# Seven block products in a gated cell: a first sum held in three PSUM tiles, the fifth product's bank reused, the second sum moved behind the sixth

## Chip, core and metric

One core of a Trainium2 chip runs the whole problem. The metric is the device time in microseconds, the median of three runs: 1669.55 us (1669.16 to 1672.69). The names of engines are those of the profile: PE is TensorE's matmul, PEld its weight load, DVE is VectorE, ACT is ScalarE, POOL is GpSimd, SP the queue that issues most DMAs.

## What is computed

The input is `x`, 64 graphs of 256 nodes with 256 features, and `adj`, 64 matrices of 256 x 256. After a layer norm and a ReLU, each graph goes through two convolutions along the nodes, through a message product with an affinity matrix, and then through a gated cell, which is where the change lies. All is in float32.

```
h = max(layernorm(x), 0)
x_conv = relu(bn(conv17(relu(bn(conv1(h))))) + h)
A = exp(-dist(h @ w_se)) * adj
x_nmp = A @ relu(h @ w_msg + b_msg)
gi = concat(x_conv, x_nmp) @ w_ih.T + b_ih        # 768 columns: r, z, n
gh = h @ w_hh.T + b_hh
r = sigmoid(gi_r + gh_r);  z = sigmoid(gi_z + gh_z)
n = tanh(gi_n + r * gh_n)
out = x + (1 - z) * n + z * h
```

## The kernel before

**Work and stages.** Two graphs (G = 2, 512 columns side by side) are a pair; 32 pairs are taken in 8 blocks of four. Features lie on the partitions, in two halves of 128. The wide convolution is done with a hand-written transform, whose additions run on DVE; its products stream filter weights from DRAM into the slots `wb`. A block's loop body (lines 1331 to 1495) lists, pair by pair, embedding, affinity, aggregation, convolution, `sums` and `gates`.

**The seven products.** A gate's pre-activation for a pair is a 2 x 2 block product: two feature halves in, two out (dc 0 and dc 1), with the two graphs as the other block index. It is done with seven block products in place of eight (`seven`, line 1162). `sums` (line 1104) forms the block sums of the inputs on DVE in slots of `wb`; `weight_sums` forms those of the weights once, in `w_x`. One call of `part(p, k, ...)` (line 1140) is product k, added up over the inputs h, xn and xc into 512 columns of PSUM: the 256 columns of one gate and the 256 of the other. `seven` is called for the gates r and z (unit RZ, three inputs for each of two gates, six matmuls a part) in all 32 pairs, and for n (unit NH, three matmuls a part) in the first 31; the last pair has an order of its own (lines 1237 to 1253), which the change leaves alone.

**Where the sums lie.** PSUM is cut into four tiles of one bank, `aux`, and two tiles of two banks, `acc`; both are rings that hand out tiles in the order of the program text (lines 580 and 581). In `seven`, `A` and `E` are `acc` tiles and the fifth product `p5` an `aux` tile. The steps are: product 1 into `A[:, 0]`; ACT writes its negative into `E[:, 0]`; product 5 into `p5`, which ACT copies to the slot `e`; product 2 onto `A[:, 0]`; product 6 onto `E[:, 0]`; DVE adds `E[:, 0]` and `e` into `A[:, 1]` (line 1174, below "the add"); product 7 onto `E[:, 0]`, which the add has just read; DVE writes `E[:, 1]` (line 1176); product 3 onto `A[:, 1]`; product 4 onto `E[:, 0]`. `opened(0, A)` and `opened(1, E)` then read both graphs of one half at a time: for RZ two ACT tanh of 128x512 each (`rz`, line 1192), for NH an ACT affine and an ACT copy of 128x512 each (`n`, line 1197).

**What sets the order.** All operations go through a recorder (line 250). Before they are emitted, a planner (line 395) orders each engine's instructions by simulated time from a table of costs: at each moment an engine takes what is ready, by due time (`late`), so a matmul of another stage can be put where the next one would wait. Due times on PE follow the text. For PSUM the planner knows only whole tiles (lines 279 and 280), so the two banks of an `acc` tile are one thing to it. On the chip each engine then runs its own list in order. `between` (line 1424 and the like) is work listed between RZ and NH of a pair: in the first and third pair of a block it holds `affinity` (line 1027), which takes four `aux` tiles at once for four small matmuls (`zT`), recorded as one task; ACT then takes four exponentials from them and DVE four products with `adj`.

All recorded operations are shown at line 378 (those small matmuls at 374), so groups are told apart by the tiles they write and read: `acc<-wb,w_x` is product 7, `aux<-wb,w_x` product 5, `acc<-hT,w_x`, `acc<-xnm,w_x` and `acc<-Yv,w_x` product 3, `acc<-wb,w_hh` and `acc<-wb,w_ih` products 6 and 4, `acc<-hT,w_hh` and its like products 1 and 2. The profile counts each float32 matmul as two records.

## Time and profile before

| | |
|---|---|
| median of three runs | 1669.55 us |
| profiled execution, its own time | 1671.88 us |
| span of the profiled execution | 1670.1 us |
| PE busy | 1645.7 us, 99% of the span |
| DVE busy | 1456.8 us, 87% |
| ACT busy | 1127.2 us, 67% |
| POOL busy | 236.0 us, 14% |
| mean granted TensorE clock | 0.997 |
| product 7, PE idle before its matmuls | 7.8 us |

The span runs from the first to the last instruction; 1.8 us of the profiled execution's time lie around it. "Busy" is the sum of the times in which an engine has at least one instruction running; for PE the ends are modelled, so a start that comes late can show partly as busy time of the matmul before it. "Idle before" is the time in which the engine had nothing running just ahead of an instruction, with the instruction whose signal ended it.

### The profile page before, as it was taken

What the parts mean: (1) busy time and instruction counts of PE and PEld (TensorE: products, weight loads), DVE (VectorE), ACT (ScalarE), POOL (GpSimd) and SP (SyncE); (2) the same over time, 40 slices, a digit from 0 to 9 for tenths busy, and PEclk for the clock granted to TensorE, in tenths of its full rate; (3) what the DMA queues carried; (4) which work ended last, traced back from release to release, by engine and by line L of the source; (5) the groups of instructions that cost most, each with busy time, mean ns of one, the idle gap of its engine ahead of it and who ended that gap; (6) DMA issues with size and microseconds to landing.
All of it is one profiled execution on the core that took longest, in us unless ns stands there. A gap on an engine that the chain in (4) does not pass through costs nothing.

```text
span 1670.1 us, 26281 instructions
## 1 busy us (share of the span) xinstructions
PE 1645.7 (99%) x8984; PEld 1413.3 (85%) x8984; DVE 1456.8 (87%) x3401; ACT 1127.2 (67%) x2029; POOL 236.0 (14%) x245
## 2 busy tenths in 40 slices
PE   9999999999999999999999999999999999999997
PEld 6888878978899788988889887897889978898886
DVE  7979989889889898898998988988988989789544
ACT  5546766776767767686756776677676776657554
POOL 4210210022110221103110131002211022000000
PEclk9999999999999999999999999999999999999999
DMA  9882557856468455783478654684647845375022
GB/s 250 301 291 75 135 109 203 264 110 147 108 202 227 105 123 126 237 205 95 114 139 265 151 122 103 176 259 110 146 108 207 222 108 133 83 231 142 16 61 51
DMA packets 314936, 261.37 MB, mean 156 GB/s; under 512 B 192875, under 2 KB 240263, under 8 KB 314802
## 3 DMA queue, kind: packets, MB, share of 16 engines
q1 hardware_dynamic: 297010, 216.71, 48.9%
q0 software_dynamic: 17376, 42.66, 11.3%
q8 instruction: 71, 1.16, 0.3%
q14 instruction: 63, 0.52, 0.1%
q10 hardware_dynamic: 416, 0.32, 0.1%
HBM read 156.60 MB, written 43.78 MB: 120 GB/s over the span
## 4 chain that ended last, share of the span: by engine, by line
PE 70%; DVE 24%; DMA 3%; issue 2%; ACT 1%; SPq 0%; DVEq 0%; ACTq 0%
PE acc L378 49%; PE aux L378 21%; DVE V L378 5%; DVE tr L378 3%; DVE U L378 3%; DVE T L378 3%; DVE wb L378 3%; DVE acc L378 2%; DVE gn L378 2%; DMA wb<-filt 2%; DVE st L378 1%; DVE PT L378 1%; DVE msg L378 1%; PE aux L374 1%; DVE Sv L378 0%
## 5 line engine op out<-in xcount | busy, mean ns | idle before, releaser
L378 PE MATMUL acc<-wb,w_ih 128*128 128x256 f32 x768 | 191.9, 379 | 0.0
L378 PEld LDWEIGHTS acc<-wb,w_ih 128*128 128x128 f32 x768 | 145.9, 190 | 19.8
L378 POOL DMA_DIRECT2D back<-in_x_dram x62 | 56.5, 1051 | 727.7 <-ACT back L378 379.5
L378 POOL TENSOR_TENSOR rstd<-rstd,neg_half 128x4 f32<-128x4 f32 x32 | 85.8, 2682 | 458.5 <-DVE shift L378 272.5
L378 PE MATMUL acc<-wb,w_x 128*128 128x256 f32 x576 | 136.9, 383 | 7.8 <-DVE acc L378 7.8
L378 ACT COPY back<-tr 128x512 uint16<-128x512 uint16 x124 | 128.3, 1078 | 22.5 <-DVE tr L378 22.2
L378 DVE SCALAR_TENSOR_TENSOR V<-T,V 128x128 f32<-128x128 f32 (+2 forms) x448 | 141.1, 379 | 0.0
L378 PE MATMUL aux<-wb,w_x 128*128 128x256 f32 x576 | 138.1, 382 | 0.0
L378 PEld LDWEIGHTS acc<-wb,w_x 128*128 128x128 f32 x576 | 106.9, 190 | 36.3 <-DVE acc L378 17.7
L378 PEld LDWEIGHTS aux<-wb,w_x 128*128 128x128 f32 x576 | 108.7, 191 | 17.3 <-DVE wb L378 2.6
L378 PE MATMUL aux<-w_msg,hT 128*128 128x259 f32 x512 | 121.7, 381 | 0.0
L378 PE MATMUL acc<-V,wb 128*128 128x128 f32 x1024 | 118.5, 275 | 0.8 <-DMA wb<-filt 0.8
L378 PEld LDWEIGHTS acc<-U,wb 128*128 128x128 f32 x1024 | 116.9, 192 | 2.6 <-ACT acc L378 1.7
L378 PE MATMUL acc<-U,wb 128*128 128x128 f32 x1024 | 117.2, 275 | 1.6 <-DMA wb<-filt 1.6
L378 PEld LDWEIGHTS acc<-V,wb 128*128 128x128 f32 x1024 | 116.4, 192 | 1.3 <-DMA wb<-filt 1.2
L378 ACT ACTIVATE gn<-acc,bn_columns 128x512 f32<-128x512 f32 (+1 forms) x64 | 43.5, 680 | 106.6 <-PE acc L378 101.5
L378 PE MATMUL acc<-Yv,w_ih 128*128 128x256 f32 x380 | 108.4, 381 | 2.1 <-ACT Yv L378 2.1
L378 PE MATMUL acc<-wb,w_hh 128*128 128x256 f32 x384 | 109.4, 380 | 0.7 <-ACT acc L378 0.7
L378 PEld LDWEIGHTS aux<-w_msg,hT 128*128 128x128 f32 x512 | 96.5, 190 | 14.3
L378 ACT COPY back<-gn 128x1024 uint16<-128x1024 uint16 x62 | 82.8, 1342 | 36.3 <-DMA gn<-back 36.3
L378 PE MATMUL aux<-hT,w_c 128*128 128x512 f32 x224 | 106.1, 592 | 0.0
L378 PE MATMUL acc<-hT,w_hh 128*128 128x256 f32 x380 | 104.0, 380 | 0.0
(200 smaller groups left out, 3898.3 us busy)
## 6 DMA issues: line engine op xcount, KB each, us to landing
wb<-filt SPq DMA_DIRECT2D x348, 256.0 KB
back<-in_x_dram POOLq DMA_DIRECT2D x62, 256.0 KB, 5.0
out_dram<-back POOLq DMA_DIRECT2D x62, 256.0 KB, 2.9
x<-in_x_dram SPq DMA_DIRECT2D x58, 256.0 KB
halves_d<-halves SPq DMA_DIRECT2D x28, 512.0 KB
adjh<-halves_d SPq DMA_DIRECT2D x112, 128.0 KB
hh<-halves SPq DMA_DIRECT2D x108, 128.0 KB
filt<-Yv POOLq DMA_DIRECT2D x18, 224.0 KB, 4.4
```

The lines of the kernel that those rows point to most:

```text
L374: self.tasks[k].call.append(lambda: method(*args, **kw))
L378: self.tasks.append(Task(engine, [lambda: method(*args, **kw)], cost, size, self.first))
```

## The change

The first sum's two graphs no longer share an `acc` tile. `a0` is the first bank of an `acc` tile (its second bank stays unused), and `a1` is the `aux` tile that held the fifth product: once ACT has copied it to `e`, the add writes its sum over it. Product 2 moves behind product 6 and the add in the text. The readers of the first half then have two separate tiles to read, so each of their ACT instructions of 128x512 becomes two of 128x256. `E` stays as it was.

```diff
     def seven(i, unit, opened):
 
-        A = acc()
-        part(A[:, 0], 1, i, unit, True)
+        a0 = acc()[:, 0]
+        part(a0, 1, i, unit, True)
         E = acc()
-        nc.scalar.mul(E[:, 0], A[:, 0], -1.0)
-        p5 = aux()
-        part(p5, 5, i, unit, True)
+        nc.scalar.mul(E[:, 0], a0, -1.0)
+        a1 = aux()
+        part(a1, 5, i, unit, True)
         e = slots[ROLE["e"]].rearrange("p c d -> p (c d)")
-        nc.scalar.copy(e, p5)
-        part(A[:, 0], 2, i, unit)
+        nc.scalar.copy(e, a1)
         part(E[:, 0], 6, i, unit)
-        nc.vector.tensor_add(A[:, 1], E[:, 0], e)
+        nc.vector.tensor_add(a1, E[:, 0], e)
+        part(a0, 2, i, unit)
         part(E[:, 0], 7, i, unit)
         nc.vector.scalar_tensor_tensor(E[:, 1], E[:, 0], -1.0, e, op0=ALU.mult, op1=ALU.subtract)
-        part(A[:, 1], 3, i, unit)
-        opened(0, A)
+        part(a1, 3, i, unit)
+        opened(0, (a0, a1))
         part(E[:, 0], 4, i, unit)
         opened(1, E)
 
-    def halfs(p, k):
-        return p[:, :, k * N:(k + 1) * N]
-
-    def pieces(t):
-        return t.rearrange("p (g n) -> p g n", n=N)
+    def halfs(t, p, k):
+        if isinstance(p, tuple):
+            return [(t[:, g * N:(g + 1) * N], p[g][:, k * N:(k + 1) * N]) for g in range(G)]
+        return [(t.rearrange("p (g n) -> p g n", n=N), p[:, :, k * N:(k + 1) * N])]
...
         def rz(dc, p):
             for gate, t in ((0, tr[:, dc]), (1, tz[dc])):
-                nc.scalar.activation(pieces(t), halfs(p, gate), AF.Tanh,
-                                     bias=b_rz[:, gate * DC + dc:gate * DC + dc + 1], scale=0.5 - dc)
+                for o, v in halfs(t, p, gate):
+                    nc.scalar.activation(o, v, AF.Tanh, bias=b_rz[:, gate * DC + dc:gate * DC + dc + 1],
+                                         scale=0.5 - dc)
 
         def n(dc, p):
             g = gn[:, dc]
-            nc.scalar.activation(pieces(g), halfs(p, 1), AF.Identity,
-                                 bias=b_hh[:, 2 * DC + dc:2 * DC + dc + 1], scale=1.0 - 2 * dc)
+            for o, v in halfs(g, p, 1):
+                nc.scalar.activation(o, v, AF.Identity, bias=b_hh[:, 2 * DC + dc:2 * DC + dc + 1],
+                                     scale=1.0 - 2 * dc)
             x = XNM[i][:, dc]
-            nc.scalar.copy(pieces(x), halfs(p, 0))
+            for o, v in halfs(x, p, 0):
+                nc.scalar.copy(o, v)
```

## The prediction, as made before the result was known

> **What bounds the kernel now.** I read the shares of busy time first, then the waits of PE, then the row of product 7, and last the timeline around one of its waits. The first three lines are from the page: busy time, and the chain of work that ended last.

> ```profile
> PE 1645.7 (99%) x8984; PEld 1413.3 (85%) x8984; DVE 1456.8 (87%) x3401; ACT 1127.2 (67%) x2029; POOL 236.0 (14%) x245
> ...
> PE 70%; DVE 24%; DMA 3%; issue 2%; ACT 1%; SPq 0%; DVEq 0%; ACTq 0%
> ...
> L378 PE MATMUL acc<-wb,w_x 128*128 128x256 f32 x576 | 136.9, 383 | 7.8 <-DVE acc L378 7.8
> ```

> PE has 24.4 us without work in 1670.1, so it is the bound nearly throughout, and no edit that leaves its matmuls alone can win more than that. The chain's 24% for DVE doesn't contradict it: DVE is nearly as full, and the chain runs through it where PE starts late by tenths of a microsecond. The waits of PE itself (waiter, what ended the wait, total us, times, longest) say what the 24.4 us hold:

> ```profile
> PE acc L378 <- DVE acc L378: 7.8, 18, 0.7
> PE aux L378 <- DVE U L378: 3.6, 2, 3.4
> PE acc L378 <- DMA wb<-filt: 2.4, 2, 1.6
> PE acc L378 <- ACT Yv L378: 2.1, 1, 2.1
> ```

> The largest, 7.8 us in 18 waits, is the idle time of product 7's row: it overwrites `E[:, 0]` and must wait until the add has read it. One such place, PE and DVE in the timeline (start, duration, then the group):

> ```profile
> 950.46 1.89 PE L378 MATMUL acc<-wb,w_ih 128*128 128x256 f32 x8
> ...
> 952.11 0.75 DVE L378 BATCH_NORM_STATS2 st<-x 128x6 f32<-128x256 f32 x2
> ...
> 952.28 0.71 PE L374 MATMUL aux<-zT 9*128 9x256 f32 x8
> 952.77 0.69 DVE L378 TENSOR_TENSOR acc<-acc,wb 128x512 f32<-128x512 f32 x1
> ...
> 953.51 0.70 PE L378 MATMUL acc<-wb,w_x 128*128 128x256 f32 x2 [0.52 <-DVE acc L378]
> ```

> Product 6 ends at about 952.2; DVE, busy with statistics, starts the add at 952.77 and ends it at 953.46, and product 7 starts at 953.51. Between lie only the four small `zT` matmuls. At another place the planner found a wider filler:

> ```profile
> 966.99 0.59 PE L378 MATMUL acc<-wb,w_ih 128*128 128x256 f32 x2
> ...
> 967.42 1.88 PE L378 MATMUL aux<-hT,w_c 128*128 128x512 f32 x4
> 967.70 0.70 DVE L378 TENSOR_TENSOR acc<-acc,wb 128x512 f32<-128x512 f32 x1 [2.98 <-PE acc L378]
> ...
> 969.14 1.46 PE L378 MATMUL acc<-wb,w_x 128*128 128x256 f32 x6
> ```

> Here the add starts 0.28 us after the sixth product, is over at 968.40, and PE doesn't stop.

> [...]

> **The move of product 2.** It is 12 records in RZ and 6 in NH, PE only, without a DMA or another queue. The matmul starts of product 4 give the price of one product:

> ```profile
> 958.80 1.03 PE L378 MATMUL acc<-wb,w_hh 128*128 128x256 f32 x4
> 959.66 1.89 PE L378 MATMUL acc<-wb,w_ih 128*128 128x256 f32 x8
> 961.39 0.59 PE L378 MATMUL acc<-hT,w_hh 128*128 128x256 f32 x2
> ```

> 961.39 - 958.80 = 2.59 us for RZ, so half, 1.30 us, for NH. Moved between 6 and 7 it covers the add. The two kernels' instruction lists as built let me count what stands there. Before, of the 64 sets of seven (the last pair's included), 47 have 1.30 us or more of other matmuls, 16 have only the `zT` group and one a single transpose. That is 17 short covers for 18 waits, so of 47 covers of 1.30 us or more just one was too short. After, all 64 have at least 1.30 us: 32 exactly 2.59 (RZ), 18 exactly 1.30, 14 more than 1.30 by a filler besides. The need is about 1.1 us where DVE is free (0.28 to the start, 0.70, some 0.1 back) and 1.3 at the place above. So I take the 7.8 us down to about 0.6: 18 covers at the bare 1.30, some 3 of them short by 0.2. Gain 7.2 us. The fillers that stood there aren't lost, they only run elsewhere on a full PE.

> **Products 1, 5 and 6.** Product 6 now follows 5 with nothing between. It needs ACT's negation of the first sum; so did product 2 before, at the same place, so the wait isn't new. In NH the cover is product 5, 1.30 us, against 0.2 + 0.59 + 0.1 = 0.9 us for the negation (586 ns in its row); 20 sets of NH stand so bare in the new list. It also needs the block sums of the inputs from DVE 1.30 to 2.59 us sooner after product 5 than before; these follow the previous pair's product 4, with 5.2 us of products 1 and 5 between, for 3.5 us of DVE work (six sums, 3 x 0.68 + 3 x 0.42). Bounds: 0 and 20 x 0.3 = 6 us; I take 0.5, since the planner puts in fillers where it sees a wait, and its 47 covers were nearly all enough.

> **The bank of product 5.** Before, `p5` was free once ACT had copied it; now it is held through 6, 2, 7 and 3 and their readers, some 11.5 us in RZ (4 x 2.59 + 1.1). The ring's fourth next user is the last tile of the affinity group, so `zT` waits for the readers of `a1`: the list shows it moved from between 6 and 7 to the middle or the end of product 4. Those readers take 0.2 + 2 x 0.47 = 1.1 us after product 3, and product 4 offers 1.3 to 2.6 us. I price it at 0, cover named; without it 16 waits of up to 1.1 us. In return `a0`'s `acc` tile frees after product 2's readers instead of product 3's; I count nothing for that, as no wait on `acc` tiles of any size is in the list of waits.

> **ACT.** 64 tanh more (32 RZ) and 62 affines and copies (31 NH). Busy time: 64 x (2 x 0.474 - 0.685) + 31 x (0.948 - 0.687) + 31 x (2 x 0.405 - 0.578), with 405 ns from the 256-column copy `V<-acc`, = 16.8 + 8.1 + 7.2 = 32 us. ACT goes from 67% to 69%. None of it is on PE's path while its results come before PE needs the tile; the readers of `a0` can even start two products earlier. DVE: the same number of adds at the same price, 0.

> **The sum.** 1671.88 - 7.2 + 0.5 = 1665.2 us for an execution like the profiled one. That is 6.7 us, or 0.4%; from the median of the runs, 2.3 us lower than the profiled one, 1669.55 - 6.7 = 1662.8 us. A change under 0.2% (3.3 us) a measurement of this kernel can't tell from none.

> **Rivals.** *The add is late anyway* (same): at the 18 bare covers DVE's list decides. If it is behind by 0.3 us in each, 5 us come back, and 1667.8 us is left. For it: DVE is 87% busy, and the add above started 0.5 us late. Against: 25 covers of 1.30 us before made hardly a wait. *ACT at the seam of RZ and NH* (slower): in two pairs of four `zT` now ends beside product 4, so behind it ACT holds two tanh of 512 for dc 1 (0.575 us apart), four exponentials (1.21 us together) and then NH's negation; before, the exponentials were over two products earlier. By rows the negation ends 3.0 us after product 4, PE needs it at 3.3 to 3.5. If one copy of `adj` (1.35 us) or of the affine results gets ahead of it, PE waits 0.9 us; in 16 seams 14.4 us, and the end is 1662.8 + 14.4 = 1677.2 us. It decides from 16 waits of 0.42 us on, that is from ACT 0.8 us late at each. Against: the new list puts negation ahead of the fourth exponential and of those copies. *More gain* (faster still): in the last block PE waits 2.1 us for `Yv` and then runs 3.4 us at half clock; a shifted order could spare that, 1662.8 - 4 = 1658.8 us. The list still has that wait, so little for it. That the change doesn't do what it says is excluded by the list.

> **Chances.** Forecast 0.63, late add 0.18, seam 0.14, more gain 0.05. Faster by over 0.2%: 0.68; within: 0.18; slower: 0.14. The range leaves out the seam and the far end of more gain: 1658.5 to 1669.5; the forecast's own is 1660 to 1666.

> **What would show it.** Product 7's row with under 1.5 us of idle time and the first line of PE's waits gone; `tr<-acc` and `tr<-aux` of 256 at about 474 ns; ACT near 69%; PE's busy time unchanged within 3 us. Wrong it would be if PE shows a new wait on ACT (`acc<-acc` ahead of product 6, or the readers of `a1` ahead of `zT`) of 3 us or more in total, or if product 7 still waits for the add.

## The result, and the profile after

The changed kernel takes 1672.78 us (median of 20 runs, 1667.02 to 1677.49), the kernel before 1670.06 us on the same chip (20 runs, 1668.98 to 1672.69). The ratio is 1.0016, with a 95% interval of 1.0009 to 1.0022: 2.7 us slower, where 6.7 us faster had been forecast. The profiled execution of the changed kernel happens to be the shortest of its 20: 1667.02 us, near the 1665.2 us that the prediction's sum gave for an execution. The loss lies in the others, so I profiled the same kernel three times more (1672.17, 1670.68 and 1674.83 us) and read all four.

The page of the changed kernel, first profile, with the lines that answer those of before, and the rows of products 5 and 6:

```profile
PE 1644.6 (99%) x8984; PEld 1411.5 (85%) x8984; DVE 1459.5 (88%) x3401; ACT 1146.3 (69%) x2155; POOL 242.6 (15%) x245
...
PE 75%; DVE 16%; DMA 4%; issue 2%; ACT 2%; SPq 1%; POOL 1%; ACTq 0%; DVEq 0%
...
L378 PE MATMUL aux<-wb,w_x 128*128 128x256 f32 x576 | 137.1, 380 | 2.2 <-DVE wb L378 2.2
L378 PE MATMUL acc<-wb,w_x 128*128 128x256 f32 x576 | 135.1, 380 | 0.0
...
L378 PE MATMUL acc<-wb,w_hh 128*128 128x256 f32 x384 | 105.0, 382 | 5.1 <-ACT acc L378 3.1
```

Product 7's row has no idle time left (7.8 us before). The time before products 5 (2.2 us) and 6 and 4 (5.1 us, which were 0.7 before) is new. The waits of PE in the same profile (waiter, what ended the wait, total us, times, longest):

```profile
PE acc L378 <- ACT acc L378: 3.1, 1, 3.1
PE aux L378 <- DVE wb L378: 2.2, 6, 0.5
...
PE acc L378 <- DVE acc L378: 1.9, 4, 0.9
```

The third line was the 7.8 us of the add. It now holds other waits: product 4 behind the write of `E[:, 1]`. The place that the change was meant for looks as the prediction drew it (PE and DVE in the timeline):

```profile
945.22 1.13 PE L378 MATMUL aux<-wb,w_x 128*128 128x256 f32 x4 [0.28 <-DVE wb L378]
...
948.78 1.03 PE L378 MATMUL acc<-hT,w_hh 128*128 128x256 f32 x4
...
949.42 0.70 DVE L378 TENSOR_TENSOR aux<-acc,wb 128x512 f32<-128x512 f32 x1
...
951.37 0.81 PE L378 MATMUL acc<-wb,w_x 128*128 128x256 f32 x3
```

The add runs from 949.42 to 950.12 while product 2 runs (948.78 to 951.37), and product 7 follows it without a stop. But product 5 has just waited 0.28 us for an input sum.

**Where the time went.** Since the ends of matmuls are modelled, I took all starts on PE, subtracted from each distance the usual one (0.216 us a record of 256 columns, 0.429 of 512, 0.112 of 128), and put every excess of more than 0.1 us down to the product that came late. A wait counts here with some 0.1 us more than its idle time: the add's 18 waits, 7.8 us by idle time, are 9.6. Means in us:

| excess ahead of | before, 2 profiles | after, first profile | after, 3 further | `after_late` (below) |
|---|---|---|---|---|
| product 7 (the add) | 9.6 | 0.0 | 0.4 | 0.0 |
| product 5 (input sums) | 0.9 | 3.3 | 3.9 | 1.0 |
| products 6 and 4 | 1.0 | 6.0 | 6.8 | 0.6 |
| TensorE at half clock | 1.2 | 0.0 | 2.3 | 1.3 |
| `zT` and fixed places | 15.8 | 15.9 | 16.5 | 15.3 |
| all the rest | 14.2 | 13.3 | 14.1 | 13.7 |
| sum | 42.7 | 38.5 | 44.0 | 31.9 |
| own time of these executions | 1671.2 | 1667.0 | 1672.6 | 1661.0 |

The sums move as the times do (+1.3 against +1.4 from before to the three further profiles). So the 9.2 us that were to be won were won, and 3.0 + 5.8 + 1.1 us came in at products 5, 6 and 4 and by the clock.

**Product 6 in the first block.** ACT and PE in the second pair, first profile after:

```profile
201.89 1.35 ACT L378 COPY back<-gn 128x1024 uint16<-128x1024 uint16 x1 [3.83 <-DMA gn<-back]
...
203.54 1.36 ACT L378 COPY hT<-hh 128x1024 uint16<-128x1024 uint16 x1 [0.30 <-DMA hh<-halves]
...
204.44 1.46 PE L378 MATMUL aux<-wb,w_x 128*128 128x256 f32 x6
...
204.76 0.68 ACT L378 ACTIVATE tr<-acc,b_rz 128x512 f32<-128x512 f32 x1
...
207.09 1.34 ACT L378 COPY back<-gn 128x1024 uint16<-128x1024 uint16 x1
...
208.39 0.60 ACT L378 ACTIVATE acc<-acc 128x512 f32<-128x512 f32 x1
...
209.04 0.70 PE L378 MATMUL acc<-wb,w_hh 128*128 128x256 f32 x2 [3.15 <-ACT acc L378]
```

ACT stands idle 3.83 us for a transfer (`gn<-back`), with the tanh of RZ's second half and the negation listed behind. RZ's second half was complete on PE at 199.6, and its tanh starts at 204.76. Four wide copies of about 1.3 us are then ahead of the negation, which starts at 208.39; product 5 has ended at about 205.7, and PE stands still for 3.15 us. The same two ACT instructions in the kernel before:

```profile
198.44 1.33 ACT L378 COPY back<-gn 128x1024 uint16<-128x1024 uint16 x1
...
207.98 0.58 ACT L378 ACTIVATE acc<-acc 128x512 f32<-128x512 f32 x1
```

There the copy ran 9.5 us ahead of the negation. SP had issued that transfer at 192.80; after the change it issues it at 194.22, behind a transpose of `hh` at 190.29 in place of 186.21, because ACT gives the normalised `hh` at 187.7 to 190.3 in place of 184.1 to 186.2. ACT itself waits there 1.86 us for `shift` from POOL, whose instruction ends at 187.67 (177.97 before; times on POOL are rough). The transfer took 7.7 us from issue to the copy, against at most 5.6.

**Product 4 in the later blocks.** SP, DVE and PE, second profile of the same changed kernel (`again`):

```profile
606.56 0.63 SPq L378 DMA_DIRECT2D x<-in_x_dram  x1
...
612.08 0.43 DVE L378 BATCH_NORM_STATS2 st<-x 128x6 f32<-128x256 f32 x1 [1.90 <-DMA x<-in_x_dram]
...
612.44 1.02 PE L378 MATMUL aux<-hT,w_c 128*128 128x512 f32 x2
...
613.82 0.69 DVE L378 SCALAR_TENSOR_TENSOR acc<-acc,wb 128x512 f32<-128x512 f32 x1
...
614.57 0.70 PE L378 MATMUL acc<-wb,w_hh 128*128 128x256 f32 x2 [1.11 <-DVE acc L378]
```

DVE is held 1.90 us by the statistics, whose `x` has not landed. Behind them in its list stand a short step of the transform, two input sums and then the write of `E[:, 1]`, which frees `E[:, 0]` for product 4. PE's fillers are over before that, and it waits 1.11 us. The place comes back in five later blocks (near 414, 612, 810, 1008 and 1206 us). In all four profiles of the change PE's wait there is DVE's wait for `x` less about 0.8 us (1.99 gives 1.20, 1.02 gives 0.23), and none where `x` was late by less than that.

The kernel before has the same statistics at the same place of DVE's list, four instructions ahead of the write, and DVE doesn't wait there (SP and DVE):

```profile
603.45 0.70 SPq L378 DMA_DIRECT2D x<-in_x_dram  x1
...
611.17 0.42 DVE L378 BATCH_NORM_STATS2 st<-x 128x6 f32<-128x256 f32 x1
```

So DVE's order is not what is new. The load takes about as long as before: by its semaphore it has landed 5.2 us after its issue there (608.62) and 5.5 us after it in `again`. But SP issues it at 606.56 in place of 603.45, behind a transpose of `hh` that holds SP for 5.68 us (4.90 before), while DVE comes to the statistics at 610.18 in place of 611.17. A margin of 2.5 us (611.17 - 608.62) has become a wait of 1.90.

### The profile page after: what moved, and what is told of

It reads as the page before. It is cut to its first block, busy times and chain, and to the rows that moved or that the text cites. A ratio compares the mean times of both kernels' runs of the same rounds, so it can differ in the third digit from the quotient of the medians.

```text
span 1665.2 us, 26516 instructions
## 1 busy us (share of the span) xinstructions
PE 1644.6 (99%) x8984; PEld 1411.5 (85%) x8984; DVE 1459.5 (88%) x3401; ACT 1146.3 (69%) x2155; POOL 242.6 (15%) x245
## 4 chain that ended last, share of the span: by engine, by line
PE 75%; DVE 16%; DMA 4%; issue 2%; ACT 2%; SPq 1%; POOL 1%; ACTq 0%; DVEq 0%
PE acc L378 48%; PE aux L378 26%; DVE V L378 4%; DVE T L378 3%; DMA x<-in_x_dram 2%; DVE wb L378 2%; DMA hh<-halves 1%; SPq L378 1%; PE aux L374 1%; DVE tr L378 1%; DVE Yv L378 1%; DVE e L378 1%; DMA wb<-filt 1%; DVE U L378 1%; DVE st L378 1%
## 5 line engine op out<-in xcount | busy, mean ns | idle before, releaser
L378 PE MATMUL acc<-wb,w_ih 128*128 128x256 f32 x768 | 188.9, 380 | 0.0
L378 PEld LDWEIGHTS acc<-wb,w_ih 128*128 128x128 f32 x768 | 145.3, 190 | 21.8 <-issue 2.3
L378 POOL DMA_DIRECT2D back<-in_x_dram x62 | 56.7, 1059 | 732.6 <-ACT back L378 592.7
L378 POOL TENSOR_TENSOR rstd<-rstd,neg_half 128x4 f32<-128x4 f32 x32 | 79.2, 2474 | 431.8 <-DVE shift L378 273.7
L378 DVE SCALAR_TENSOR_TENSOR V<-T,V 128x128 f32<-128x128 f32 (+2 forms) x448 | 141.4, 383 | 0.0
L378 ACT COPY back<-tr 128x512 uint16<-128x512 uint16 x124 | 130.2, 1076 | 15.7 <-DVE tr L378 15.3
L378 PE MATMUL aux<-wb,w_x 128*128 128x256 f32 x576 | 137.1, 380 | 2.2 <-DVE wb L378 2.2
L378 PE MATMUL acc<-wb,w_x 128*128 128x256 f32 x576 | 135.1, 380 | 0.0
L378 PEld LDWEIGHTS aux<-wb,w_x 128*128 128x128 f32 x576 | 108.6, 190 | 22.1 <-DVE wb L378 5.0
L378 PEld LDWEIGHTS acc<-wb,w_x 128*128 128x128 f32 x576 | 109.0, 190 | 18.6 <-issue 1.7
L378 PEld LDWEIGHTS acc<-U,wb 128*128 128x128 f32 x1024 | 118.2, 192 | 2.3 <-DMA wb<-filt 1.1
L378 PE MATMUL acc<-U,wb 128*128 128x128 f32 x1024 | 119.0, 275 | 0.9 <-DMA wb<-filt 0.9
L378 PE MATMUL aux<-w_msg,hT 128*128 128x259 f32 x512 | 118.6, 381 | 0.0
L378 PE MATMUL acc<-V,wb 128*128 128x128 f32 x1024 | 118.5, 275 | 0.0
L378 PEld LDWEIGHTS acc<-V,wb 128*128 128x128 f32 x1024 | 116.4, 192 | 0.5 <-DMA wb<-filt 0.4
L378 PE MATMUL acc<-wb,w_hh 128*128 128x256 f32 x384 | 105.0, 382 | 5.1 <-ACT acc L378 3.1
L378 PEld LDWEIGHTS aux<-w_msg,hT 128*128 128x128 f32 x512 | 95.9, 190 | 14.1
L378 DVE TENSOR_TENSOR e<-e,adj 128x256 f32<-128x256 f32 x128 | 68.8, 595 | 44.2 <-ACT e L378 43.9
L378 PE MATMUL aux<-hT,w_c 128*128 128x512 f32 x224 | 105.0, 593 | 0.1
L378 PE MATMUL acc<-Yv,w_ih 128*128 128x256 f32 x380 | 102.7, 379 | 2.1 <-ACT Yv L378 2.1
L378 PE MATMUL acc<-hT,w_hh 128*128 128x256 f32 x380 | 104.6, 381 | 0.0
L378 PE MATMUL acc<-xnm,w_ih 128*128 128x256 f32 x380 | 103.5, 379 | 0.0
```

What stands on the lines that cost most here:

```text
L378: self.tasks.append(Task(engine, [lambda: method(*args, **kw)], cost, size, self.first))
```

## The experiments

My theory was that the planner's lists are at fault: it takes a transfer as landed 1.1 us after its data have passed (`plan`, line 445), puts instructions that wait for transfers ahead of others on ACT and DVE in that trust, and the shifted lists of the change have less slack where the trust is wrong. The rivals: the split readers on ACT cost the time; the ring of tiles does (`a1` held for longer); or the half-clock stretches do, with waits as before. Where an expectation uses letters, P stands for the planner's figure being too early for any kernel, D for the waits in the lists, S for the split readers, C for the clock.

**`again`**: the changed kernel, unaltered.

> The changed kernel, unaltered, to see an execution nearer its median than the one profiled first (span 1665.2 us, the fastest of 20; the 20 ran from 1667.0 to 1677.5, those of before from 1669.0 to 1672.7). Theory D (late transfers): in the new order ACT copies and DVE statistics that wait for transfers stand ahead of the negation, of the input sums or of the write of E[:, 1], so a transfer that lands 1 to 3 us later than the planner thought reaches PE. It expects a span of 1669 to 1675 us, with product 7 still nearly free of waits (under 1.5 us), and 4 to 8 us more PE waits on ACT and DVE ahead of products 5, 6 and 4 than in the fast execution. Theory C (clock): the same waits as in the fast execution, and one to four more stretches at half clock[...]. Theory S (split readers): every execution pays, no difference between a fast and a slow one is explained.

Measured: 1672.17 us (21 runs, 1669.01 to 1677.53), ratio 1.0012 (1.0005 to 1.0019). The small loss is real, and so is the spread: 8.5 us here and 10.5 in the first series, against 3.7 to 6.7 for the kernel before.

**`tiles_only`**: the three tiles, with product 2 ahead of 6 as it was.

```diff
+        part(a0, 2, i, unit)
         part(E[:, 0], 6, i, unit)
         nc.vector.tensor_add(a1, E[:, 0], e)
-        part(a0, 2, i, unit)
```

> Three tiles as in the change, but product 2 ahead of product 6 in the text, as before. As built, 60 of 64 adds have 1.3 us or more of other matmuls behind them, 4 have less, none of the zT sort; product 6 again has product 2 between it and product 5 wherever the planner likes. If it is the move of product 2 that takes the slack from what product 6 waits for (D in its narrow form), this gives 1662 to 1665 us with a scatter of under 4 us. If the lost time comes from what the tiles do to the order of ACT and SP (D in its wide form), or from the split readers (S), it stays at 1670 to 1675 us with the scatter of the change.

Measured: 1680.1 us (1679.74 to 1681.04), ratio 1.0058 (1.0044 to 1.0071). PE's waits:

```profile
PE aux L378 <- ACT e L378: 8.0, 12, 1.0
```

Without the move, product 5 of NH gets the tile of a `zT` that has just been made, and waits until ACT has taken the exponential from it: eight of the twelve waits and 7.3 of the 8.0 us are of this kind. Product 7's wait for the add is nearly gone here too (2.6 us by starts), so what the tiles cost in this order is more than the 10 us of loss: by starts product 5 has 9.0 us of excess and product 1 and its like 7.1, where the kernel before has 0.9 and 2.3. In the change itself none of this is seen.

**`split_only`**: the kernel before, with the readers of the first half split.

```diff
-        opened(0, A)
+        opened(0, (A[:, 0], A[:, 1]))
```

(with the new `halfs`, `rz` and `n` of the change)

> The kernel before with its first half's readers split into two graphs each, nothing else: 126 more ACT instructions, tiles and text order as before. Theory S: 3 us or more slower than before, 1673 us or over. Theory D: within 2 us of before either way, ACT about 19 us busier, product 7 waiting for the add as before (about 8 us).

Measured: 1671.79 us (13 runs, 1670.44 to 1674.5), ratio 1.0012 (1.0003 to 1.002). ACT has 1141.0 us busy, the add's waits are the 7.8 us in 18 of the kernel before, and there is no new wait at product 6 above 1.2 us. The split costs about 1.7 us by the medians, too little for the 9 us that came in.

**`after_late`**: the change, with the planner taking each transfer as landed 1.5 us later.

```diff
-                t.done = self.dma + 1.1
+                t.done = self.dma + 2.6
```

> The change, with a planner that believes every transfer lands 1.5 us later than it did, so that it puts what waits for transfers later in the lists of ACT and DVE. Theory D: the waits of ACT, DVE and PE that go back to transfers shrink, the scatter falls to that of before (4 us over all runs), and the median comes to 1662 to 1667 us. Theories S and C: 1671 to 1675 us, as the change.

Measured: 1659.72 us (1658.73 to 1661.02), ratio 0.9937 (0.9924 to 0.9949), the fastest version of all. The same place in the first block:

```profile
201.25 0.68 ACT L378 ACTIVATE wb<-acc,b_rz 128x512 f32<-128x512 f32 x1
202.12 1.35 ACT L378 COPY back<-gn 128x1024 uint16<-128x1024 uint16 x1 [0.19 <-DMA gn<-back]
...
206.32 0.62 ACT L378 ACTIVATE acc<-acc 128x512 f32<-128x512 f32 x1
...
207.00 0.70 PE L378 MATMUL acc<-wb,w_hh 128*128 128x256 f32 x2 [0.33 <-ACT acc L378]
```

The transfer is no earlier (202.1 against 201.9): SP issues it at 194.45. But RZ's tanh now stand ahead of the copy that waits for it, and the negation ends 2.05 us sooner (206.94 against 208.99), though product 5 starts 0.77 us later; 0.33 us of wait are left of 3.15. The waits for transfers, first of `after_late`, then of the change:

```profile
ACT back L378 <- DMA gn<-back: 9.5, 11, 3.7
DVE st L378 <- DMA x<-in_x_dram: 4.3, 2, 3.6
```

```profile
ACT back L378 <- DMA gn<-back: 18.4, 10, 3.8
DVE st L378 <- DMA x<-in_x_dram: 12.0, 9, 3.7
```

The kernel before has 36.3 us (15) and 4.6 us (3) in these lines: more waiting for `gn<-back` than either, at no loss. So not their sum counts, but what is listed behind them.

In the later blocks it is SP's list that differs: here SP issues `x` at 596.86, ahead of the transpose of `hh` at 598.27, and the statistics at 606.25 find it landed. It is so in all five blocks. Of the 12.1 us between the last two columns of the table above, 9.1 are at products 5, 6 and 4.

**`before_late`**: the same edit of the planner in the kernel before.

> The kernel before with the planner that lands every transfer 1.5 us later: the control to the change with that planner, which took 1659.7 us. The change's own worth, once transfers are no matter, is the difference of the two. Theory D with the prediction's step for the add right: before has little to gain from this planner, since its waits on PE are the 7.8 us for the add, so it stays at 1666 to 1671 us and keeps these waits; the change's worth is then 7 to 10 us. If the late planner alone is what gained (theory P), this gives 1660 to 1663 us and the change is worth nothing.

Measured: 1677.13 us (1674.2 to 1678.14), ratio 1.0037 (1.0025 to 1.005), slower where I had expected faster or no change. Its waits:

```profile
PE acc L378 <- DVE acc L378: 5.7, 17, 0.7
...
PE aux L378 <- DVE wb L378: 3.9, 7, 0.9
```

The add's waits are still there, product 5's are new, and by starts it has 4.8 us at half clock. So the later figure isn't better as such (P falls): it is worth 12.5 us to the changed kernel (1672.17 to 1659.72) and costs the one before 7. The pair of lists and change is what counts.

**`after_late_x` and `after_late_rest`**: the later landing for the loads of `x` alone, and for all other transfers alone.

```diff
-                t.done = self.dma + 1.1
+                t.done = self.dma + 1.1 + (1.5 if k in self.slow else 0.0)
```

(`self.slow` holds the transfers into `x`, or all others)

> The change, with only the loads of x believed 1.5 us later (they are waited for by the statistics on DVE, ahead of the input sums and of the write of E[:, 1]). Theory D says that two kinds of lateness reach PE: statistics behind x on DVE (some 6 us of PE waits in the steady blocks) and copies behind hh and gn on ACT (3 us in the first block). If x is the main one: median 1663 to 1667 us, the repeating waits before products 4 and 5 gone, the 3 us wait of product 6 in the first block still there. If not: 1669 us or over.

> The complement: all transfers but the loads of x believed 1.5 us later. If x is the main cause: 1667 to 1671 us, with statistics still waiting 10 us or more for x on DVE. If the copies on ACT are: 1662 to 1665 us.

Measured: 1667.32 us (14 runs, 1663.75 to 1671.68), ratio 0.9989 (0.9981 to 0.9997), and 1662.64 us (1659.66 to 1664.61), ratio 0.9953 (0.9941 to 0.9964). With `x` alone the waits that come back in each block are gone, and product 6's wait in the first block stays (3.5 us). The rest alone gives most of the gain. But the pair doesn't part the kinds of transfer cleanly. With the rest alone SP too issues `x` ahead of the transpose of `hh` (599.88 and 601.27), so DVE's waits for `x` fall to 5.5 us in 4, though the figure for `x` is that of the change; with `x` alone the statistics stand behind the write of `E[:, 1]` instead (631.50 and 617.46).

**`after_later`**: all transfers 3.0 us later.

```diff
-                t.done = self.dma + 1.1
+                t.done = self.dma + 4.1
```

> The change, with every transfer believed 3 us later. Theory D: waits on transfers are gone already with 1.5 us, so no more is won, 1658 to 1664 us, by what the planner loses in other places for having to put copies later. A median under 1657 us would say that 1.5 us was not enough of a margin.

Measured: 1672.32 us (19 runs, 1669.8 to 1674.14), ratio 1.0013 (1.0006 to 1.0019). A miss. The waits of DVE for `x` are as few as in `after_late` (4.1 us in 2), but the starts hold 11.6 us more than there, for 12.0 us more in the profiled executions. Of these 3.7 us are in the groups of `zT`: in eight of them (one in `after_late`) PE stops between the four small matmuls, six times for ACT's copies of their input, and the group at 493.73 takes 1.29 us in place of 0.71. Products 5, 6 and 4 have 1.6 us more, the half clock 1.5, product 1 and its like 1.2, and the rest is in small pieces. More margin is not better; the lists differ everywhere.

**`after_late_b0` and `after_late_b1`**: the 1.5 us for the transfers issued up to the end of the first block, and for those of the later blocks.

> The change, with the transfers of the prologue and the first block alone believed 1.5 us later; from the second block on the lists are almost those of the change. Theory D: the 3 us wait of product 6 in pair 1 (ACT's negation behind copies whose transfers landed late) shrinks to 1.5 us or less and with it goes the half-clock stretch that it can bring, so the median falls by 3 to 5 us to 1667 to 1669 us, and the scatter (8 to 10 us in the change) to 5 us or less; the repeating waits before products 4 and 5 stay. Against D: no difference, 1671 us or over.

> The complement: the first block planned as in the change, later blocks with transfers believed 1.5 us later. Theory D: the 3 us wait of pair 1 stays, with its half-clock stretch in a part of the executions, so the scatter stays at 7 us or more; the waits repeated in each block (about 1 us a block, six blocks) go, and the median is 1663 to 1667 us. The two parts' gains should come to about the 12.5 us of the whole.

Measured: 1668.18 us (19 runs, 1664.15 to 1673.85), ratio 0.9984 (0.9975 to 0.9993), and 1664.92 us (1664.24 to 1668.3), ratio 0.9973 (0.9961 to 0.9984). The first loses the 3 us wait of product 6, and keeps product 5's 4.2 us and the waits for `x`; the second the other way round (product 6's is 2.8 us, product 5 has 0.8). From `again`, 4.0 and 7.3 us, of 12.5 for both: the two parts nearly add up (11.3). I had the spread wrong: it stays at 9.7 us in the first, and is 4.1 in the second (7 runs only). It seems to go with the later blocks.

**`tiles_only_late`**: `tiles_only` with the 2.6 us of `after_late`.

> Three tiles, product 2 ahead of product 6, and the planner that lands every transfer 1.5 us later. With the planner as it was, this kernel took 1680.1 us, and its waits were not on transfers but on the exponentials of the affinity group, whose tile product 5 of NH takes next (8.0 us in 12 waits). If moving product 2 behind the add is what spares that, this stays at 1670 us or over with these waits, against 1659.7 us for the change with this planner; if the tiles alone are what counts and the 1680 us were late transfers, it comes to 1660 to 1665 us.

Measured: 1690.0 us (1688.13 to 1690.89), ratio 1.0116 (1.0102 to 1.013), and the exponential's waits are still there (7.3 us in 8). Beside `after_late` only the place of product 2 in the text differs, with the lists that the planner makes from it, and that is 30 us; the exponential's waits are a part of it, and the rest isn't traced here.

**`look2`, `look3`, `b0_look2`, `before_look2`**: one further profile each of the change (twice), of `after_late_b0` and of the kernel before, to tell waits from clock.

> A third look at the change, unaltered, for what an execution above the fastest holds. Theory C (clock carries most of the loss): two or three stretches at half clock before the tail, and waits of PE like those of the fastest execution. Theory D (late transfers carry it): one stretch or none more, and 4 us or more of added PE waits on ACT and DVE before products 4, 5 and 6. [...]

> A fourth look at the change, unaltered, with the same expectations as the third: C wants half-clock stretches and unchanged waits, D wants 4 us or more of added waits before products 4, 5 and 6.

> A second look at the change with the first block's transfers alone believed later, whose executions still scattered over 9.7 us, to see what varies. D: the waits in the repeating blocks (before products 4 and 5) differ from look to look by 1 us or more each; C: half-clock stretches differ, the waits don't.

> A second look at the kernel before. D and C both expect its waits to be those of the first look within 0.2 us each (7.8 us for the add, in 18 waits), with one half-clock stretch or none in the last block: its lists wait on transfers where nothing of PE hangs on it.

Measured: 1670.68, 1674.83, 1669.36 and 1670.43 us. The excess at products 5, 6 and 4 is in every profile of the change (9.3, 11.0, 9.8 and 11.3 us), and 1.8 to 2.0 in both of the kernel before. Half-clock time is 0, 1.3, 2.9 and 2.8 us in the change, 1.3 and 1.0 before. So the waits carry most of the loss, and the clock adds a part that varies; neither accounts for the spread alone.

## Why the prediction was wrong

- **Product 7's wait: right.** 7.8 us in 18 waits were to fall to 0.6; the row shows 0.0 in the first profile (by starts 9.6 to between 0 and 1.2). Counting the covers of 1.30 us in the lists was enough.
- **ACT: right in its share, wrong in its size.** 69% as forecast, but 19.1 us more busy time for the 32 worked out. I had added durations: by the rows of the kernel before 685 ns for `tr<-acc,b_rz` of 512 columns, 474 for `gn<-acc,bn_columns` of 256, 405 for the copy. Neighbouring instructions overlap on ACT: of two tanh of 256 columns that start at 198.03 and 198.40 in `after_late` each lasts 0.47. Two starts 0.37 us apart in place of one 0.58 us before the next make 2 x 0.37 - 0.58 = 0.16 us for each of the 64 tanh and 31 affines, and 2 x 0.252 - 0.466 = 0.04 us for each of the 31 copies: 16 us, between the 13.8 of `split_only` and the 19.1. Prices of one instruction held for the tanh (472 ns for 474), less well for the copies (365 for 405). DVE's add kept its price: 694 ns before, into `acc`, and 698 after, into `aux`.
- **The bank of product 5: right as priced, 0.** `zT` and the fixed places went from 15.8 to 15.9 and 16.5 us. Its price where the order doesn't cover it is `tiles_only`'s.
- **"Products 1, 5 and 6", 0.5 us with bounds of 0 and 6: this step failed.** It measured 3.0 us more at product 5, 5.8 at 6 and 4, and some 1 us at half clock (1.2 before, 2.3 in the three further profiles). It failed in two ways. I compared the need with the compute of ACT and DVE alone (0.9 us for a negation, 3.5 us for six sums) and left out what stands ahead of the work in their lists: a copy or a statistic that waited for a transfer held all behind it, 3.83 us on ACT and 1.90 us on DVE above. And "the planner puts in fillers where it sees a wait" was no protection: by its code (line 445) the planner takes such a transfer as landed, so the wait isn't in its time. The prediction's own sign of being wrong, a new wait on ACT of 3 us or more ahead of product 6, came with 3.1 us.
- **Product 4 wasn't in the prediction.** Moving product 2 away from ahead of 6 leaves everything else of a set where it was, I thought. In DVE's list it does: the statistics stood ahead of the write of `E[:, 1]` before as well. What I had no term for is that DVE comes to them sooner and SP issues their `x` later, so that a margin of 2.5 us was used up.
- **Product 5's waits**, up to 0.5 us each in the list of waits, are plain lateness of DVE (it is busy without a gap ahead of 945.22). The prediction names this need, but counted its bound of 6 us over 20 bare sets of NH; these six are in RZ, one a block. They are back to the size of before in `after_late` and `after_late_b1` (1.0 and 0.8 us by starts), whose DVE lists differ.
- **The seam rival** named the right mechanism, a copy on ACT ahead of the negation, but put it at 16 seams at 0.9 us each; it happened at one, in the first block, for 3.1 us. "The new list puts negation ahead of [...] those copies" is true of the seams that I had looked at, not of this pair.
- **The 24.4 us without work were no ceiling.** By starts the kernel before loses 42.7 us, since a late start can hide behind a modelled end; `after_late` wins 10.
- **From the profiled execution to the median.** The sum was made for one execution, and that one came near it (1667.0 for 1665.2) by luck: the failed step cost 7.4 us in it too, and the execution, the shortest of 20, had no stretch at half clock before its last 7 us. That the spread would grow from some 4 to 7 us to 8 to 10, so that the median of the changed kernel lies 5.8 us above its shortest run, I had no term for.

What stays open: what sets the size of the spread from one execution to the next, and whether any other reshuffling of the lists would have gained as much. No run changes the lists by something that has nothing to do with transfers; that the landing time did it is read from the waits that go with it. That the lists of the planner and not the change's own cost decide is shown by one line that turns +2 us into -10; that 2.6 is a good figure for anything but this pair is not shown, and `before_late` speaks against it.

## What to carry to other kernels

An edit that frees one wait on a full engine also gives a planner a new list for every other engine, so ask of each instruction on the freed path what stands ahead of it in its engine's list, whether any of that waits for a transfer, and what stands ahead of that transfer in the queue that issues it. An engine that comes to a place sooner can find late a transfer that used to be in time: here DVE came 0.99 us sooner (610.18 for 611.17) to a load issued 3.11 us later (606.56 for 603.45), and waited 1.90 us. What stood ahead in these lists cost by the transfer's lateness: 3.83 us of waiting on ACT stood ahead of PE's 3.15, where the compute alone was 0.9 us with 1.30 us of cover. Give the planner a landing time that the trace supports, but measure it, since another margin helps one version and hurts the next (1.5 us more won 12.5 us in the changed kernel and lost 7 in the one before). And take several profiles when two versions differ in spread: the shortest execution of the changed kernel showed 4 us of gain (1667.0 against 1671.2) where the median lost 2.7.

## What the runs showed of the hardware

In `again` product 6's wait of 2.77 us, which ends at 208.41, is followed by a stretch at half clock. The windows behind it (after PE, PEld, DVE, ACT and POOL come the granted clock, the DMA share and GB/s):

```profile
210.00:211.00 1.00, 1.00 (x4) 0.81 (x3) 0.83 (x2) 1.00 (x3) 0.00 (x0) 0.50 1.02 249
...
213.50:215.00 1.50, 1.50 (x8) 1.19 (x7) 0.69 (x1) 0.43 (x1) 0.36 (x1) 1.00 0.98 112
```

The stretch is 3.41 us long (209.75 to 213.16) and costs 1.3 us in the count by starts. In the kernel before, PE's wait of 2.09 us for `Yv`, which ends at 1538.03, is followed by one of the same length (1538.50 to 1541.91, clock 0.50). In the first profile of the change the wait of 3.15 us at product 6 has none: the clock is 1.00 from 205 to 217 us. So the length of the wait alone didn't decide.
